# A conditioned transformer block on one core: seven second-level Strassen products in three ff residuals, none in the ssm residuals

## The chip, the core and the metric

The kernel runs on one core of a Trainium2 chip, in fp32. The core has TensorE (PE in the profile), VectorE (DVE), ScalarE (ACT) and GpSimd (POOL), each with a queue of its own, and SyncE (SP), from whose queue most DMAs are issued. An engine takes its instructions strictly in the order in which the program lists them. The metric is the device time of one execution in microseconds (us).

## The reference

Two sequences of 2048 tokens with 512 channels, `x` (2, 2048, 512); each has a row of conditions `t` of 512 numbers, from which six rows of shift, scale and gate are made.

```python
emb = dot(silu(t), ada_w) + ada_b
shift_msa, scale_msa, gate_msa, shift_mlp, scale_mlp, gate_mlp = split(emb, 6)
norm = ln(x) * (1 + scale_msa) + shift_msa
h = gelu(dot(norm, ssm_w1) + ssm_b1)              # 512 x 512, exact gelu
x = x + gate_msa * (dot(h, ssm_w2) + ssm_b2)      # 512 x 512
norm2 = ln(x) * (1 + scale_mlp) + shift_mlp
hf = gelu_tanh(dot(norm2, ff_w1) + ff_b1)         # 512 x 1024
return x + gate_mlp * (dot(hf, ff_w2) + ff_b2)    # 1024 x 512
```

Tokens depend on each other in nothing. The gates differ for the two sequences and are multiplied into the second weights (`w2`, `fw2`), which are therefore loaded and folded twice, once for each sequence.

## The kernel before

**Blocks and stages.** The 4096 tokens are cut into eight blocks of 512 (0 to 3 belong to the first sequence, 4 to 7 to the second). Each block has four matmul stages, and the names of tiles in the profile carry them: *hA* is the ssm hidden product (class `First`), *oA* the ssm residual, *hC* the ff hidden product (class `Second`, `products`), *oC* the ff residual. A loop over i from 1 to 7 puts the stages of neighbouring blocks in turn: hC of block i, oA of block i+1, oC of block i, hA of block i+2. While PE multiplies for one block, the other engines normalize, transpose and form sums for another.

**Strassen-Winograd.** A plain product of two matrices cut into quarters takes eight products of quarters. The Winograd form takes seven, P1 to P7, and pays with sums: four of each operand beforehand (`sums_of_first` for activations, `sums_of_second` for weights, which both give the third and fourth sum as the third and fourth entry of a list), and adds of the results, which DVE makes from PSUM into `x` in place (`residual`, L795). A product of quarters is P1, P2 and so on in the code, and several of them accumulate in one PSUM bank. The banks' tags are y, x, v and t, each with two buffers. At the start of a residual two banks are filled by ACT with the bias row (`seed`), so that the bias comes with the first add. After P1 ACT copies bank y to a new bank x (the order named CARRIED).

**The second level.** In a residual, a product can itself be done by the same form: its quarter matrices are cut into quarters again, and seven *leaves* of 128 columns are multiplied instead of eight. The leaves of the several products that are done so run in rounds: round 0 computes leaf P1 of each of these products, round 1 leaf P2, and so on in the order of `LEAVES`; after a round (but for round 0) DVE adds the results to `x`. Before the change, the ff residuals of blocks 1 to 7 do five of their seven products in leaves (`residual_in_leaves`: P2, P3, P4, P5 and P7; P1 and P6 are plain, L897 the plain matmul, L945 that of a leaf, L959 the adds of leaves). The ssm residuals of blocks 3 to 6 (i from 2 to 5) do P2, P3 and P4 in leaves (`residual_with_leaves`: L832 plain, L847 leaf, L862 adds of leaves), the others none (L495 in `group`, the matmul of `residual` and `First`). The leaf sums of activations are made by POOL on line L349 (a line of `cut_sum`), in the constant tile `forms`, which also holds the registers of the ff hidden product.

**The ff hidden product** has a longer table of sums (`HK_P`, `HK_A`, `HK_B`) and 26 products, which DVE (L1140) and ACT (L1137) collect. Its operands are made by POOL ahead of it from the 'registers' of the normalized block (L1047).

**The order of the work** is written by hand: there is no scheduler. A stage is a list of matmuls, and a dictionary `hooks` says after which product (a number for hC; P1, P2, R0 and so on for the others) the operations of other engines are put into their queues. Whatever the place, each engine takes its own operations in the order of the code, so a hook's place decides what an operation stands behind on its engine. A hook at P5 of a CARRIED stage stands at the place of the fourth product of the usual order.

**The layer norm of a block** goes through these steps: statistics on DVE (L533) or ACT, `root` (a variance on DVE, L603, and a power of -1/2 on POOL, L575), `steps` or `rest` (five small operations on DVE, L607 to L611), `normal` on ACT (L626), `turn` on DVE (L637, a transpose within 32x32 blocks), `move` (16 DMAs, L646), `moved` (ACT's modulate, L669, in place) and at last the sums of the result on POOL.

**Loads.** The tiles of x, h and the normalized blocks come from one pool of seven buffers (`big_tile`); a new tile takes a buffer that became free. `load_x` (L203) brings in a block's x, `load_half` (L221) half of `fw2`, both on SP. Block 4 begins the second sequence. For it `w2` is loaded again and folded with the new gate at i = 2 (`refold2`), and `fw2` at i = 3 (`refold5`; folds on DVE, L397); the bias rows are multiplied by the gates in `gate_bias` (L1023, with L478 for the difference of its halves).

## Time and profile before

| what | value |
|---|---|
| median of three runs | 586.86 us (586.22 to 587.11) |
| profiled execution | 585.99 us |
| its span | 584.2 us |
| PE busy | 576.8 us, 3375 instructions |
| DVE busy | 447.3 us, 891 instructions |
| POOL busy | 422.0 us, 462 instructions |
| ACT busy | 274.1 us, 512 instructions |

The span runs from the first to the last instruction in the trace, the execution's time a little around it. An engine that is busy for nearly all of the span sets the time as long as it isn't kept waiting, so the wait of that engine is what to look for. In a line of the timeline the first number is the start in us from the beginning of the span, the second the length of the group of like instructions in a row, then the engine, the line of the kernel, the operation, the tile written and the tiles read, their shapes, and how many instructions the group has; in square brackets stand idle time just before and what ended it. In a line of groups, the numbers behind the bar are the busy time of all in us and the mean of one in ns. The steady stages of the loop begin, in PE's timeline, at 153.77 (oA of block 2), 165.86 (oC of block 1), 200.78 (hC of block 2), 223.23 (oA of block 3), 234.83 (oC of block 2), 257.37 (hA of block 4), 304.18 (oC of block 3), 326.71 (hA of block 5), 361.31 (oA of block 5) and 454.28 (oC of block 5).

### The profile page before, as it was taken

To read this page: it belongs to the slowest core of one execution; us is meant where nothing else is said; L and a number is where in the kernel's file an instruction comes from. 1 tells how busy PE (TensorE), PEld (TensorE's weight loads), DVE (VectorE), ACT (ScalarE), POOL (GpSimd) and SP (SyncE) were. 2 spreads that over 40 slices of the span, in tenths; PEclk is the share of its full clock that TensorE was granted. 3 is DMA by queue.
4 is the path that set the end of the run, shared out by engine and by line. 5 is a ranking of instruction groups with operands and counts; after the bars stand their busy time and mean duration, and the time that the engine had idled before them with its cause. 6 is when DMAs were issued, how large, how long until landed. Compare 5 with 4: busy or idle time off the path is not lost.

```text
span 584.2 us, 9795 instructions
## 1 busy us (share of the span) xinstructions
PE 576.8 (99%) x3375; PEld 516.4 (88%) x3375; DVE 447.3 (77%) x891; ACT 274.1 (47%) x512; POOL 422.0 (72%) x462
## 2 busy tenths in 40 slices
PE   8999999999999999999999999999999999999996
PEld 5888888888889889998899988998889998899896
DVE  4978898996878576896967678986766487887676
ACT  2234357705642655535733588235665331732520
POOL 1875349999949788599968999997770593369350
PEclk9999999999999999999999999999999999999999
DMA  8990422302205303353032920252130240031002
GB/s 317 395 383 6 109 65 82 108 37 108 56 19 144 145 1 69 116 168 119 1 92 59 312 81 22 51 136 105 49 73 2 96 121 1 0 74 73 0 1 74
DMA packets 25246, 56.52 MB, mean 97 GB/s; under 512 B 4672, under 2 KB 5740, under 8 KB 23532
## 3 DMA queue, kind: packets, MB, share of 16 engines
q1 hardware_dynamic: 21856, 51.67, 27.7%
q10 hardware_dynamic: 3340, 4.22, 2.9%
q8 instruction: 27, 0.44, 0.3%
q14 instruction: 23, 0.19, 0.1%
HBM read 32.80 MB, written 8.40 MB: 71 GB/s over the span
## 4 chain that ended last, share of the span: by engine, by line
PE 92%; DVE 3%; DMA 2%; POOL 1%; issue 1%; SPq 0%; ACT 0%; DVEq 0%; POOLq 0%
PE px_hC L1123 10%; PE py_hA L495 9%; PE py_oC L897 8%; PE pv_hC L1123 8%; PE py_hC L1123 8%; PE pl_oC_P_y L945 8%; PE py_oA L495 5%; PE pl_oC_P_v L945 5%; PE pv_hA L495 4%; PE py_oA L832 3%; PE pl_oC_P_x L945 3%; PE pv_oA L495 2%; PE py_hC L495 2%; PE py_oC L495 2%; PE px_hA L495 2%; PE pv_oC L945 2%
## 5 line engine op out<-in xcount | busy, mean ns | idle before, releaser
L575 POOL TENSOR_TENSOR r<-ve,minus_half 128x4 f32<-128x4 f32 x16 | 16.6, 1036 | 60.5 <-DVE pl_oC_P_v L603 34.0
L669 ACT ACTIVATE nT<-nT,mod,mod 128x512 f32<-128x512 f32 x32 | 23.4, 804 | 57.6 <-DMA nT<-blocks 34.6
L1047 POOL TENSOR_TENSOR forms<-forms 128x256 f32<-128x256 f32 x56 | 42.1, 752 | 4.2 <-DVE forms L1043 0.7
L532 DVE BATCH_NORM_STATS2 st<-x 128x6 f32<-128x512 f32 x56 | 37.9, 677 | 4.9 <-DMA x<-in_x_dram 4.7
L1123 PE MATMUL py_hC<-forms,fw 128*128 128x256 f32 x168 | 41.2, 380 | 0.4 <-DVE hClo L1140 0.4
L349 POOL TENSOR_TENSOR hSC<-hClo,hChi 128x512 f32<-128x512 f32 (+1 forms) x16 | 19.0, 1192 | 26.4 <-ACT hChi L1118 22.9
L1140 DVE TENSOR_TENSOR hClo<-hClo,py_hC 128x512 f32<-128x512 f32 x42 | 28.6, 684 | 11.0 <-ACT hClo L1137 8.5
L1123 PEld LDWEIGHTS py_hC<-forms,fw 128*128 128x128 f32 x168 | 31.6, 190 | 5.4 <-DVE hClo L1140 1.0
L669 ACT ACTIVATE x<-x,mod,mod 128x512 f32<-128x512 f32 x24 | 17.6, 802 | 34.3 <-DMA x<-blocks 34.3
L1140 DVE TENSOR_TENSOR hChi<-hChi,pv_hC 128x512 f32<-128x512 f32 x35 | 23.2, 680 | 8.0 <-PE pv_hC L1123 6.5
L1118 ACT ACTIVATE hClo<-hClo,colsT 128x256 f32<-128x256 f32 x56 | 25.3, 499 | 5.0 <-DVE hClo L1140 4.8
L1123 PE MATMUL px_hC<-forms,fw 128*128 128x256 f32 x112 | 27.6, 379 | 0.0
L626 ACT ACTIVATE nT<-x,nmr,rstd 128x512 f32<-128x512 f32 x32 | 23.7, 804 | 6.2 <-POOL nmr L590 3.7
L959 DVE TENSOR_TENSOR x<-pl_oC_P_y,x 128x256 f32<-128x256 f32 (+1 forms) x66 | 24.7, 374 | 2.2 <-PE pl_oC_P_y L945 0.6
L637 DVE STREAM_TRANSPOSE blocks<-nT 128x512 f32<-128x512 f32 x32 | 22.4, 708 | 5.0 <-ACT nT L626 5.0
L1118 ACT ACTIVATE hChi<-hChi,colsT 128x256 f32<-128x256 f32 x56 | 25.1, 496 | 1.9 <-DVE hChi L1140 1.9
L1137 ACT ACTIVATE hClo<-px_hC 128x512 f32<-128x512 f32 x21 | 12.5, 596 | 28.1 <-PE px_hC L1123 22.7
L897 PE MATMUL py_oC<-fw_s,hSC 128*128 128x256 f32 x112 | 25.3, 379 | 0.0
L897 PE MATMUL py_oC<-fw,hClo 128*128 128x256 f32 x112 | 25.3, 379 | 0.0
L349 POOL TENSOR_TENSOR hClo<-hClo 128x512 f32<-128x512 f32 (+1 forms) x23 | 24.8, 1082 | 0.0
L1123 PEld LDWEIGHTS px_hC<-forms,fw 128*128 128x128 f32 x112 | 21.3, 190 | 2.9
L959 DVE TENSOR_TENSOR x<-pl_oC_P_v,x 128x256 f32<-128x256 f32 (+1 forms) x56 | 20.3, 385 | 4.1 <-PE pl_oC_P_v L945 2.6
(403 smaller groups left out, 1839.2 us busy)
## 6 DMA issues: line engine op xcount, KB each, us to landing
x<-in_x_dram SPq DMA_DIRECT2D x13, 1024.0 KB
out_dram<-x SPq DMA_DIRECT2D x14, 512.0 KB
ada<-in_L_cond_ada_w_dram SPq DMA_DIRECT2D x6, 1024.0 KB
x<-blocks SPq DMA_DIRECT2D x96, 64.0 KB
nT<-blocks SPq DMA_DIRECT2D x80, 64.0 KB
fw<-in_L_cond_ff_w_dram SPq DMA_DIRECT2D x2, 2048.0 KB
w<-in_L_cond_ssm_w_dram SPq DMA_DIRECT2D x3, 1024.0 KB
nT<-blocks ACTq DMA_DIRECT2D x48, 64.0 KB
```

Of the source, the lines that this page charges most:

```text
L349: eng.tensor_tensor(out[:, r], a[:, r], b[:, r], f)
L495: nc.tensor.matmul(ps[b][j * apart][:, j, :], lhs(p, j, k), rhs(p, j, k), start=(fresh and j * (not apart) == 0 and k == 0), stop=(p in (" ...
L532: nc.vector.bn_stats(st, xs[self.i][:, c, :])
L626: nc.scalar.activation(t, x_c, AF.Identity, bias=self.nmr[:, c : c + 1], scale=self.rstd[:, c : c + 1])
L669: nc.scalar.activation(dst, src, AF.Identity, bias=shift, scale=scale)
L897: yield lambda j=j, k=k: nc.tensor.matmul(ps[BANK[p]][:, j, :], hops(p, j, k), wops[p][:, k, :], start=False, stop=(k == kdim - 1), skip_g ...
L945: nc.tensor.matmul(t[:, n, :], hops.leaves[p][f][:, k, :], leaf_wops[p][f][:, k, :], start=room not in started, stop=(f in ("P2", "P3", "P ...
L959: nc.vector.tensor_tensor(d, src, d, ALU.add)
L1047: eng.tensor_tensor(reg[d], reg[a], reg[b], ALU.add if f == "+" else ALU.subtract)
L1118: nc.scalar.activation(h, h, AF.Gelu_apprx_tanh, bias=fb1T[:, m : m + 1])
L1123: nc.tensor.matmul(ps[b][:, j, :], fa[ra][:, j * P : (j + 1) * P], fb[rb].rearrange("p a (c q) -> p c a q", q=Q), start=(fresh and j == 0) ...
L1140: nc.vector.tensor_tensor(dest(d), dest(d), ps[b], op)
```

## The change

Three of the ff residuals, those of blocks 2, 3 and 5 (`SEVEN`), do all seven products in leaves, in a new function; the other ff residuals keep five. All ssm residuals are plain again, so that the leaf sums for `w2` and for the ssm activations go. What the new residual needs is placed anew:

- `residual_in_all_leaves` has two groups of banks, A for P2, P4, P3, P6 and B for P5, P1, P7. In each round the leaves of A are multiplied, then those of B; DVE adds three times for A and five times for B. ACT copies round 0's banks for round 1. Hooks have names such as 0a and 2b, the round and the group.
- Four sums of the weights' quarters P1 and P6 are added. They are made in block 1's arrangement and again after the reload of `fw2`; the fourth ones are kept in room beside the leaf sums of h, which is a big tile (in block 5 the tile of `w1`), and parked in DRAM between blocks 2 and 3. The third sum is made in place in the weight and changes it for the plain use; `plain` takes that back in the blocks that come next with five products.
- Leaf sums of activations: those of P1 and P7 together (`pair_leaf_sums` on half 0), of P2 and P4 (on half 1), and of P5, P6 and P3 (`third_leaf_sums`), all on POOL.
- In these blocks the load of x three blocks on goes to the end of the residual (6b instead of P5), the store of the first half too. In block 2, `w2` is loaded at 0a instead of P1, and its folds and sums move from the residual to the hidden stage that follows and to the next ff hidden stage (`late_w2`), with the gate taken from PSUM.
- `moved` of block i+2 stands at P1 instead of R0 in the one ssm residual (i = 5) that is followed by hA.
- A hook of the folds of `fw2` after the reload goes from places 0 and 8 of the ff hidden stage to 8 alone.

The diff, cut to its core:

```diff
+        fourths, plain = [], []
+        for j, (p, w) in enumerate((("P1", lo[:, :, : D // 2]), ("P6", s[:, 1]))):
+            q, t = {n: v[:, :, 0, :] for n, v in views(w).items()}, [pair_w[:, 0, j], pair_w[:, 1, j], None]
+            ops[p] = second_operands(q, t)
+            sums[p] = sums_of_second(q, t, engs[p])[:3]
+            fourths.append((p, q["21"], t[1]))
+            plain.append(lambda q=q: nc.gpsimd.tensor_tensor(q["12"], q["22"], q["12"], ALU.subtract))
...
+    def seed_leaves(i, row):
+        by_e = row.rearrange("p (q e d) -> p q e d", q=2, e=2)
+        for b, tag, src in (("y", "x", by_e[:, :, 0]), ("v", "v", leaf_row)):
+            t = ps_g.tile([P, 3, P], F32, tag=tag, name=f"pl_oC_{i}_B_{b}")
+            seeds[f"oC_{i}", b] = t
+            nc.scalar.copy(t[:, :2], src)
+            nc.scalar.activation(t[:, 2], row[:, :P], AF.Identity, scale=0.0)
...
+    def residual_in_all_leaves(name, i, hops, leaf_wops, hooks, last):
...
+        groups = {"A": ("P2", "P4", "P3", "P6"), "B": ("P5", "P1", "P7")}
...
+        rooms = {("B", b): seeds[name, b] for b in "yv"}
+        for g, b, tag in (("A", "y", "x"), ("A", "x", "y"), ("B", "x", "y"), ("A", "v", "v")):
+            rooms[g, b] = ps_g.tile([P, len(groups[g]), P], F32, tag=tag, name=f"pl_{name}_{g}_{b}")
...
+        for r, f in enumerate(LEAVES):
...
+            for n, g in enumerate("AB"):
+                room = rooms[g, b]
+                for p in groups[g]:
+                    leaf(g, p, f)
+                if r == 0:
+                    m = len(groups[g])
+                    nc.scalar.copy(rooms[g, "x"][:, :m], room[:, :m])
+                    started.add((g, "x"))
+                elif g == "A":
+                    add(cross, room[:, 3:])
+                    add(like, room[:, 0:4:3])
+                    add(cross, room[:, 1:3])
+                else:
+                    add(like, room[:, :1])
+                    add(cross, room[:, 1:])
+                    add(last_q, room[:, 1:2])
+                    add(cross, room[:, :1])
+                    add(last_q, room[:, 2:])
+                run(hooks.get(f"{r}{'ab'[n]}", ()))
...
+    SEVEN = (2, 3, 5)
...
-            if i == 2:
-                w2_leaf, late_sums = leaves_of_w2(w2_sb, w2_s, (nc.gpsimd, nc.gpsimd))
-            if i > 1:
-                hook(hooks, (10,), hA[i + 1].leaf_sums(nc.gpsimd))
-            hook(hooks, (10,), late_sums)
...
+            if seven:
+                hook(hooks, (14, 15, 16, 17, 18, 19), wsums16)
+                wsums16 = []
+        if i - 1 in SEVEN and not seven and nxt and i != PER_B:
+            hook(hooks, (3, 5), plain_again)
...
-            hook(hooks, (0, 8), fold[:4])
+            hook(hooks, (8,), fold[:4])
...
-            hook(hooks, ("R0",) if ahead else ("P7",), n1[i + 2].moved())
+            hook(hooks, ("P1",) if ahead else ("P7",), n1[i + 2].moved())
...
-            if i == 1:
-                residual(f"oA_{i + 1}", i + 1, hA[i + 1], w2_ops, KD // 2, hooks, order=CARRIED)
-            else:
-                residual_with_leaves(f"oA_{i + 1}", i + 1, hA[i + 1], w2_ops, w2_leaf, hooks)
+            residual(f"oA_{i + 1}", i + 1, hA[i + 1], w2_ops, KD // 2, hooks, order=CARRIED)
...
+        if seven and nx2:
+            n1_sums = hA[i + 2].summed(nc.gpsimd) if ahead else n1[i + 2].summed(nc.gpsimd)
+            hook(hooks, ("0a",), [lambda: n2[i + 1].root()] + (leaf_fold or [])[:-2] + [lambda: n2[i + 1].rest()])
+            hook(hooks, ("2a", "3a"), (leaf_fold or [])[-2:])
+            hook(hooks, ("0a",), sums17[:2] + [s[2] for s in (sums24, sums356, sums17)] + n1_sums[:1])
+            hook(hooks, ("0a",), [s[3] for s in (sums24, sums356, sums17)] + fourth + n1_sums[1:])
+            hook(hooks, ("0b",), [lambda c=c: n2[i + 1].normal(c) for c in range(C)])
+            hook(hooks, ("1a", "1b", "2a", "2b"), [lambda c=c: n2[i + 1].turn(c) for c in range(C)])
+            hook(hooks, ("2b",), [lambda: n2[i + 1].move((nc.sync, nc.scalar))])
+            hook(hooks, ("3b",), n2[i + 1].moved())
...
+        if seven and i + 3 < NBLK:
+            hook(hooks, ("6b",), [lambda: load_x(i + 3)])
...
+            if seven:
+                hook(hooks, ("P6",), [lambda: found.update(gb2=bias_2())])
+                hook(hooks, ("P6", "P6", "P5", "P5", "P7", "P3", "P3", "P4"), w2_fold[:KD])
+                late_w2 = w2_fold[KD:]
```

More of the change, by code (lines that the diff above doesn't have):

```diff
@@ L429, in leaves_of_weight, with fourth @@
             sums[p] = sums_of_second(q, t, engs[p])
+        fourths, plain = [], []
[5 more added lines that the diff above has]
+            plain.append(lambda q=q: nc.gpsimd.tensor_tensor(q["12"], q["22"], q["12"], ALU.subtract))
+        def fourth(room):
+            for j, (p, a, b) in enumerate(fourths):
+                nc.gpsimd.tensor_tensor(room[:, j], a, b, ALU.subtract)
+        sums["fourth"], sums["plain"] = fourth, plain
         return ops, sums
@@ L1493 @@
                 hook(hooks, ("P1", "P2", "P6", "P5"), fold[5:6] + fold[4:5] + later[:2])
-            oC_seeds = [lambda p=p: seed(f"oC_{i}", gb[5], p, five) for p in range(2)]
+            if seven:
+                oC_seeds = [lambda: seed_leaves(i, gb[5])]
+            else:
+                oC_seeds = [lambda p=p: seed(f"oC_{i}", gb[5], p, five) for p in range(2)]
             if not ahead:
```

140 lines of the change are left out of this document (105 added, 35 removed).

## The prediction

> **What bounds the kernel.** I read the page first (busy times, then the chain that ended last), then the timeline of PE, then what PE waited for.
>
> ```profile
> PE 576.8 (99%) x3375; PEld 516.4 (88%) x3375; DVE 447.3 (77%) x891; ACT 274.1 (47%) x512; POOL 422.0 (72%) x462
> PE 92%; DVE 3%; DMA 2%; POOL 1%; issue 1%; SPq 0%; ACT 0%; DVEq 0%; POOLq 0%
> ```
>
> PE is busy for 99% of the span and carries 92% of the chain. So there are only two questions: does the change alter the number or the pace of matmuls, and does it make PE wait. The next lines are from the timeline of PE: start, length, group. Each matmul of the program shows as two instructions.
>
> ```profile
> 153.77 1.89 PE L495 MATMUL py_oA<-w,hA 128*128 128x256 f32 x8
> 155.50 1.89 PE L495 MATMUL pv_oA<-w_s,hSA 128*128 128x256 f32 x8
> 165.86 3.62 PE L897 MATMUL py_oC<-fw,hClo 128*128 128x256 f32 x16
> 169.31 0.61 PE L945 MATMUL pl_oC_P_y<-fw,hChi 128*128 128x128 f32 x4
> 169.75 0.61 PE L945 MATMUL pl_oC_P_y<-fw,hSC 128*128 128x128 f32 x4
> ...
> 223.23 1.89 PE L832 MATMUL py_oA<-w,hA 128*128 128x256 f32 x8
> ...
> 234.83 1.03 PE L897 MATMUL py_oC<-fw,hClo 128*128 128x256 f32 x4
> ...
> 257.37 0.81 PE L495 MATMUL py_hA<-x,w 128*128 128x256 f32 x3
> ...
> 304.18 2.11 PE L897 MATMUL py_oC<-fw,hClo 128*128 128x256 f32 x9
> ```
>
> Starts follow each other without holes: 16 wide instructions take 169.31 - 165.86 = 3.45 us (216 ns each), four narrow ones 0.44 to 0.45 us. What PE waited for between 60 and 574 us is two lines of the view of waits, and their places in its timeline are these:
>
> ```profile
> PE py_hC L1123 <- DVE hClo L1140: 0.4, 1, 0.4
> PE pl_oA_y L847 <- DVE x L862: 0.3, 1, 0.3
> 282.12 1.13 PE L1123 MATMUL py_hC<-forms,fw 128*128 128x256 f32 x4 [0.41 <-DVE hClo L1140]
> 369.62 0.49 PE L847 MATMUL pl_oA_y<-w,hA 128*128 128x128 f32 x2 [0.29 <-DVE x L862]
> ```
>
> With the slack of the matmul before and a slow first one behind (four wide ones take 1.13 here, 1.03 at 234.83), I put the first at about 0.6 to 0.7 us and the second, from its length and the gap, at 0.5 to 0.6. That is all that a change outside the start and the end of the kernel can win back: about 1.2 us.
>
> **The change, part by part.**
>
> *Matmuls.* A product of the ff residual costs 3.45 us plain. As seven leaves it has 28 narrow instructions: 7 x 0.445 = 3.12 us. Two more products in three blocks: 6 x 0.33 = 2.0 us won. The ssm residual takes 234.83 - 223.23 = 11.60 us with leaves and 165.86 - 153.77 = 12.09 us plain; it goes back to plain in four blocks (3 to 6): 4 x 0.49 = 2.0 us lost. Sum: 0.0. Both sides move 168 narrow and 96 wide instructions, so any other price for them gives zero too.
>
> *Vector work in the ff residual (blocks 2, 3, 5).* Before, a block has 27 adds into x; now six rounds of eight: two groups A and B, A with three adds of 256 columns, B with three of 256 and two of 128. A PE round is now 7 x 0.445 = 3.12 us (A 1.78, B 1.34). A bank is written again two rounds later, so the adds of a group in round r must end before that group starts in round r+2. Prices from the DVE timeline of block 2 and the groups by line and shape:
>
> ```profile
> 253.08 0.42 DVE L959 TENSOR_TENSOR x<-pl_oC_P_y,x 128x256 f32<-128x256 f32 x1
> 253.60 0.42 DVE L959 TENSOR_TENSOR x<-pv_oC,x 128x256 f32<-128x256 f32 x1
> 253.94 0.74 DVE L959 TENSOR_TENSOR x<-pl_oC_P_y,x 128x128 f32<-128x128 f32 x2
> 254.59 0.41 DVE L959 TENSOR_TENSOR x<-pl_oC_P_v,x 128x256 f32<-128x256 f32 x1
> L959 DVE TENSOR_TENSOR x<-pl_oC_P_y,x 128x128 f32<-128x128 f32 x22 | 6.2, 282 | 0.6 <-PE pl_oC_P_y L945 0.6
> ```
>
> An add of 256 lasts 0.42, but the next starts 0.34 after it (253.60 to 253.94); with an extra wait the step is 0.52. I take 0.34 each, 0.28 for 128 columns, 0.10 for one wait per group: A 1.12, B 1.68, a round 2.80, under PE's 3.12. Before the first round DVE ends the statistics of the ssm residual and the scales. Block 1, whose ssm residual is plain already, shows it:
>
> ```profile
> 166.06 0.69 DVE L795 TENSOR_TENSOR x<-py_oA,x 128x512 f32<-128x512 f32 x1
> 168.97 0.18 DVE L533 BATCH_NORM_AGGREGATE mv<-st 128x2 f32<-128x6 f32 x1
> 171.58 0.17 DVE L607 TENSOR_TENSOR pl_oC_P_v<-r,pl_oC_P_v 128x4 f32<-128x4 f32 x1 [0.38 <-POOL r L575]
> 172.27 0.15 DVE L611 SCALAR_TENSOR_TENSOR nmr<-mv,pl_oC_P_v 128x4 f32<-128x4 f32 x1
> 173.30 2.83 DVE L637 STREAM_TRANSPOSE blocks<-nT 128x512 f32<-128x512 f32 x4 [0.88 <-ACT nT L626]
> ```
>
> Counted from the stage's first matmul (165.86): statistics end at 3.3, the variance (0.16) and POOL's power (1.02, below) at 4.6, five small steps (0.84) at 5.4. Then, with a turn of 0.71 (2.83 / 4) behind each group of rounds 1 and 2: round 1A ends at 6.5, 1B at 8.9, 2A at 10.7, 2B at 13.1, the last turn at 13.8, 3A at 14.9, 3B at 16.6, 4A at 17.7, 4B at 19.4, 6B at 25.0. PE wants the banks of 3A at 15.6, 3B at 17.4, 4A at 18.7, 4B at 20.5: margins of 0.7, 0.8, 1.0, 1.1. Cost 0. By full lengths (A 1.36, B 1.92, a round 3.28) 3A ends at 16.2 and the waits add to about 0.9 us in blocks 2 and 3; in block 5 a whole hidden stage lies between the statistics and this residual. So bounds 0 and +1.8; I take 0, since the nearest rows are such adds and start early. DVE ends 3.2 us after PE, which the hidden stage behind it (few adds, banks read by round 5 first) takes up.
>
> *POOL.* Leaf sums of h for the ssm residual and for w2 go; sums for P1, P6 and P2, P4 wide and three P's at once come. Block 2 before:
>
> ```profile
> 231.52 1.27 POOL L349 TENSOR_TENSOR forms<-forms,hChi 128x512 f32<-128x512 f32 x1
> 239.91 1.02 POOL L575 TENSOR_TENSOR r<-ve,minus_half 128x4 f32<-128x4 f32 x1 [7.12 <-DVE pl_oC_P_v L603]
> 247.45 0.72 POOL L349 TENSOR_TENSOR hClo<-hClo 128x256 f32<-128x256 f32 x1
> 256.72 1.18 POOL L1047 TENSOR_TENSOR forms<-nT 128x256 f32<-128x256 f32 x1
> ```
>
> The idle 7.1 us before the power takes the first two sums of 768 columns (estimate 1.8 each, from 0.72 and 1.27). From the power's end at 4.6: two sums of P1/P7 to 7.1; thirds (1.27, 1.8, 1.27) to 11.5; one sum for the next hidden stage to 12.8; fourths to 14.1, 15.9, 17.2; two weight sums to 18.6; three more sums to 22.4. Round 5 reads the 768-wide fourth in its third product, at 15.6 + 0.9 = 16.5: margin 0.6, the smallest. Cost 0; if the power comes at 5.1 as in block 2 before (239.91 - 234.83, behind adds that are gone), 1.0 per block. Register sums start some 2 us later than 21.9 (256.72), since turns now sit between adds; the 12 us of a hidden stage and the first products of the next one cover them.
>
> *ACT at the stage's start.* The first leaf round comes at once instead of behind 3.45 us of a plain product, and round 1 needs ACT's copy of round 0's bank. ACT may still be at the modulates of the block after, which wait for SP's transpose DMAs:
>
> ```profile
> 292.02 11.25 SPq L646 DMA_DIRECT2D x<-blocks  x16
> 305.07 2.93 ACT L669 ACTIVATE x<-x,mod,mod 128x512 f32<-128x512 f32 x4 [8.67 <-DMA x<-blocks]
> 307.91 0.36 ACT L927 COPY pl_oC_P_v<-leaf_row 128x256 f32<-128x256 f32 x1
> 234.63 2.93 ACT L669 ACTIVATE x<-x,mod,mod 128x512 f32<-128x512 f32 x4 [7.59 <-DMA x<-blocks]
> ```
>
> In block 3 the stage will start 0.49 us later, at 304.67; ACT is free at 307.91 = 3.2, a copy of 512 columns ends at about 3.8 (estimate 0.6: 0.36 at 256, and more), round 1 wants it at 3.1: **+0.7 us**. In block 2 ACT is free 2.1 us into the stage (237.5 against 235.3): the copy ends at 2.8, 0. If the issue of its 16 DMAs takes the 11.25 us of block 3 there as well, up to 0.7; bounds 0 and +1.4, taken 0.7.
>
> *Queues.* The load of the x three blocks on moves to the end of the residual, into a buffer that only the last leaf round frees, and on SP everything behind it waits. In block 3 that is both halves of fw2:
>
> ```profile
> 321.51 0.54 SPq L203 DMA_DIRECT2D x<-in_x_dram  x1
> 323.34 1.72 SPq L221 DMA_DIRECT2D fw<-in_L_cond_ff_w_dram  x2
> 330.09 2.48 DVE L397 TENSOR_TENSOR fw<-fw,pgate 128x512 f32<-128x512 f32 x4 [2.43 <-DMA fw<-in_L_cond_ff_w_dram]
> 339.96 0.42 DVE L478 TENSOR_TENSOR gb<-gb 128x256 f32<-128x256 f32 x1
> ```
>
> x goes out 2.2 us before the stage's end instead of 5.2 (326.7 - 321.5), so the folds start some 3 us later; the slack of the lines behind them leaves about 2 us at 339.96. The next stage's first bank that waits for a DVE add is taken 6.05 us (28 x 0.216) after that stage starts, and I find 0.7 us left. Bounds 0 and +1.3; taken 0, by the idle 2.43 and what follows it. The w2 reload, its folds and the park DMA lie in stages where DVE and SP have room: 0. The late x of block 2 is read 6.9 us after it is issued at the earliest: 0.
>
> *Waits that go.* The wait at 369.62 is in the leaf form of the ssm residual, where DVE was late; plain, a bank has a product of 1.73 us between its uses: -0.56, bounds -0.56 and 0. The one at 282.12 follows the gate bias of ssm, one line of which takes 1.17 at that place and 0.42 at 339.96; it stays where it was: 0, bounds -0.65 and 0.
>
> ```profile
> 278.75 1.17 DVE L478 TENSOR_TENSOR gb<-gb 128x256 f32<-128x256 f32 x1
> ```
>
> *Sum.* 0.0 + 0.7 - 0.56 = +0.14 us. The profiled execution took 585.99 (span 584.2 and 1.8 around it), so 586.1; the median of the three runs is 0.87 above that execution: **587.0**.
>
> **Rivals.**
>
> 1. *DVE becomes the bound of the new residual* (slower, the other side). It decides as soon as a round of eight adds takes more than about 2.9 us; at full lengths it takes 3.28. For it: 27 adds become 48, and 253.08 to 253.60 is a step of 0.52. Against it: the steps of 0.34. Time: 587.0 + 1.8 = 588.8. The Trainium skill, "VectorE: DVE Perf Modes", section "The DRAIN you can't avoid", says that the next operation does not start until the pipe is empty; by that rule each add costs its full length and this rival holds. This trace does not agree for adds without a wait: 253.94 starts 0.08 us before the add at 253.60 ends.
>
> 2. *POOL and the late loads* (slower): the power at 5.1 gives 1.0 in blocks 2 and 3, the late fw2 up to 1.3, some of both waits shared: +2.5, 589.5. For it: margins of 0.6 and 0.7 in a chain of fifteen operations. Against: POOL had 7.1 us idle before the power.
>
> 3. *Both old waits go and no new one comes* (faster): -0.56 - 0.65, 585.6. For it: POOL loses the w2 leaf sums in that very stage. Against: the 2.93 us of ACT above, and the bias line stays.
>
> **How the numbers follow.** Forecast 0.50, rival 1 0.22, rival 2 0.20, rival 3 0.08. About what a measurement of this kernel can tell from no change is 0.2%, 1.2 us: the forecast and its own range (586.2 to 588.0) lie inside, rivals 1 and 2 above, rival 3 just below. So faster 0.08, same 0.50, slower 0.42. The range leaves out rival 3 and the worst of rival 2: 585.8 to 590.0.
>
> **What would show it.** In the profile after: PE with the same 3375 instructions; ff residuals of blocks 2, 3, 5 at 21.9 us plus their waits; the ssm residuals at 12.1; no wait of PE for DVE x at the sixth block; a wait of some 0.7 us for ACT's copy after the first round in block 3. Waits of PE for DVE x in rounds 5 and 6 would prove rival 1, for POOL's forms or leaves rival 2. I am wrong if one of these stages is more than 1 us longer than its matmuls, or if a hidden stage behind one shows waits.

## The result, and the profile after

The changed kernel takes 589.27 us (median of 6 runs, 587.82 to 590.34), the kernel before 586.27 on the same chip: a ratio of 1.0049, 95% interval 1.0038 to 1.0060. It is slower by 3.0 us, and its runs lie 2.5 us apart where those of before lie 0.9 apart. The profiled execution took 588.81 us with a span of 586.8, 2.6 more than before.

The busy times and the chain that ended last, of the changed kernel:

```profile
PE 577.3 (98%) x3375; PEld 515.8 (88%) x3375; DVE 443.0 (75%) x912; ACT 273.6 (47%) x509; POOL 420.3 (72%) x431
PE 84%; DVE 4%; DMA 4%; ACT 3%; SPq 2%; issue 2%; POOL 1%; DVEq 0%; POOLq 0%; ACTq 0%
```

PE has the same 3375 instructions and the same busy time within 0.5 us. Its share of the chain fell from 92% to 84%: the time came from waiting, not from multiplying. The view of PE's waits between 60 and 574 us (in all, times, longest):

```profile
PE pl_oC_A_x L1060 <- ACT pl_oC_A_x L1086: 1.0, 1, 1.0
PE py_hA L520 <- DVE hA L782: 0.7, 1, 0.7
PE pv_oA L520 <- ACT pv_oA L484: 0.4, 1, 0.4
PE py_hA L520 <- POOL forms L1128: 0.3, 1, 0.3
```

Their places in PE's timeline, with a fifth at 238.70 that shows as a slow first matmul only:

```profile
238.70 0.71 PE L1060 MATMUL pl_oC_A_x<-fw,hChi 128*128 128x128 f32 x4
268.34 1.53 PE L520 MATMUL py_hA<-nS,w 128*128 128x256 f32 x6 [0.25 <-POOL forms L1128]
309.02 0.71 PE L1060 MATMUL pl_oC_A_x<-fw,hChi 128*128 128x128 f32 x4 [1.04 <-ACT pl_oC_A_x L1086]
339.11 1.75 PE L520 MATMUL py_hA<-nS,w 128*128 128x256 f32 x7 [0.70 <-DVE hA L782]
481.27 1.56 PE L520 MATMUL pv_oA<-w_s,hSA 128*128 128x256 f32 x6 [0.42 <-ACT pv_oA L484]
```

None of the five is in a place where the kernel before had one; the two old ones are gone. What each costs is best read as the length of its stage, from the stage's first matmul in PE's timeline to that of the next one. In us:

```
stage                     before  changed  difference
oA 3, 4, 6 (each)          11.59    12.09    +0.50
oA 5                       12.15    12.09    -0.06
oC 2 (seven products)      22.54    22.25    -0.29
hA 4                       12.09    12.58    +0.49
hC 3                       23.13    22.47    -0.66
oC 3 (seven products)      22.54    23.19    +0.65
hA 5                       12.09    13.03    +0.94
hC 4                       22.50    22.75    +0.25
oC 5 (seven products)      22.54    21.88    -0.66
oA 7                       12.09    12.78    +0.69
```

They add to +2.8, and PE's last matmul ends 2.8 later (582.65 against 579.84); the other stages agree within 0.04. The ff residual of block 5 is 21.88 long, which is its matmuls and no wait. So the residuals of blocks 2 and 3 hold waits of 0.37 and 1.31.

What stands behind them, in the timelines of the other engines, ACT first:

```profile
305.56 2.93 ACT L694 ACTIVATE x<-x,mod,mod 128x512 f32<-128x512 f32 x4 [8.66 <-DMA gsb<-gates]
308.40 0.57 ACT L1086 COPY pl_oC_A_x<-pl_oC_A_y 128x512 f32<-128x512 f32 x1
477.81 2.93 ACT L694 ACTIVATE nT<-nT,mod,mod 128x512 f32<-128x512 f32 x4 [13.57 <-DMA nT<-blocks]
480.64 0.58 ACT L484 COPY pv_oA<-gb 128x512 f32<-128x512 f32 x1
```

At 309.02, ACT's copy of round 0 stands behind four modulates and ends at 308.97, 0.05 us before PE goes on at 309.02. The modulates wait for DMAs: the view names the load of the gates, which SP issues right behind the 16 transposing DMAs, and in e2 the transposing DMAs themselves. In block 5 the bias row for the next ssm residual (L484) stands behind four other modulates. DVE and, in the last two lines, SP:

```profile
264.30 2.48 DVE L397 TENSOR_TENSOR w<-w,pgate 128x512 f32<-128x512 f32 x4 [0.73 <-ACT pgate L337]
266.70 0.69 DVE L557 BATCH_NORM_STATS2 st<-x 128x6 f32<-128x512 f32 x1
267.52 0.67 DVE L782 TENSOR_TENSOR hA<-py_hA,hA 128x512 f32<-128x512 f32 x1
333.97 2.48 DVE L397 TENSOR_TENSOR fw<-fw,pgate 128x512 f32<-128x512 f32 x4 [4.40 <-DMA fw<-in_L_cond_ff_w_dram]
338.29 0.68 DVE L782 TENSOR_TENSOR hA<-py_hA,hA 128x512 f32<-128x512 f32 x1
292.26 10.30 SPq L671 DMA_DIRECT2D x<-blocks  x16
326.27 0.98 SPq L221 DMA_DIRECT2D fw<-in_L_cond_ff_w_dram  x2
```

In both hidden ssm stages the bank that P4 wants is read by L782, and L782 stands behind folds of weights: those of w2, which the change moved here, and those of fw2, whose load goes out at 326.27 (323.34 before) and whose first fold starts at 333.97 (330.09 before; the stage itself starts only 1.2 us later). The view names POOL and not DVE at 268.34, as one of POOL's sums ends near there too. It isn't POOL that PE waits for: in e2, below, the same sums of POOL come 0.5 us later (267.99 in place of 267.51), L782 0.9 us earlier, and PE doesn't wait.

### The profile page after: what moved, and what is told of

Same layout as the page of the kernel before. It is cut to its first block, busy times and chain, and to the rows that moved or that the text cites. A ratio compares the mean times of both kernels' runs of the same rounds, so it can differ in the third digit from the quotient of the medians.

```text
span 586.8 us, 9773 instructions
## 1 busy us (share of the span) xinstructions
PE 577.3 (98%) x3375; PEld 515.8 (88%) x3375; DVE 443.0 (75%) x912; ACT 273.6 (47%) x509; POOL 420.3 (72%) x431
## 4 chain that ended last, share of the span: by engine, by line
PE 84%; DVE 4%; DMA 4%; ACT 3%; SPq 2%; issue 2%; POOL 1%; DVEq 0%; POOLq 0%; ACTq 0%
PE px_hC L1204 10%; PE py_oA L520 8%; PE py_hC L1204 8%; PE py_hA L520 8%; PE pv_hC L1204 7%; PE py_oC L922 5%; PE pv_oA L520 4%; PE pl_oC_P_y L970 4%; PE pv_hA L520 3%; PE py_hC L520 2%; PE py_oC L520 2%; PE pl_oC_P_v L970 2%; PE pl_oC_A_y L1060 2%; PE px_oA L520 2%; SPq L671 2%; PE px_hA L520 2%
## 5 line engine op out<-in xcount | busy, mean ns | idle before, releaser
L520 PE MATMUL py_oA<-w,hA 128*128 128x256 f32 x112 | 26.5, 379 | 0.0
L349 POOL TENSOR_TENSOR hClo<-hClo 128x512 f32<-128x512 f32 (+1 forms) x23 | 26.2, 1141 | 0.0
L820 DVE TENSOR_TENSOR x<-py_oA,x 128x512 f32<-128x512 f32 x26 | 17.8, 686 | 10.6 <-PE py_oA L520 9.4
L820 DVE TENSOR_TENSOR x<-pv_oA,x 128x512 f32<-128x512 f32 x16 | 11.0, 686 | 17.7 <-PE pv_oA L520 9.0
L520 PEld LDWEIGHTS py_oA<-w,hA 128*128 128x128 f32 x112 | 21.1, 190 | 2.9
```

The costliest lines, as they stand in the source:

```text
L349: eng.tensor_tensor(out[:, r], a[:, r], b[:, r], f)
L520: nc.tensor.matmul(ps[b][j * apart][:, j, :], lhs(p, j, k), rhs(p, j, k), start=(fresh and j * (not apart) == 0 and k == 0), stop=(p in (" ...
L820: nc.vector.tensor_tensor(d, ps[BANK[p]][:, js], d, ALU.add)
```

## The experiments

Behind each run stand the difference of its median to that of the kernel before on the same chip ("+2.0 us") and the ratio with its interval. Single mends of less than 1 us are within the spread of the changed kernel's own runs, so that what follows from them is read from the stages' lengths and not from the medians. The lengths, in us:

```
stage   before changed  e2     e3     e4     e5     e6     e7     e8     e9     e10    e12
oC 2    22.54  22.25   22.32  22.29  22.31  21.88  22.24  22.45  22.54  22.28  21.88  21.88
hA 4    12.09  12.58   12.09  12.58  12.66  13.38  12.09  12.58  12.09  12.09  12.19  12.35
hC 3    23.13  22.47   23.26  22.47  22.47  22.46  23.45  22.47  22.93  22.97  23.29  22.68
oC 3    22.54  23.19   21.88  23.84  23.23  21.88  23.74  23.39  22.54  23.25  21.88  21.88
hA 5    12.09  13.03   13.16  12.09  13.34  13.35  12.86  13.49  12.09  12.97  12.09  12.09
oA 7    12.09  12.78   12.65  12.54  12.92  13.08  13.00  12.09  12.09  13.23  12.09  12.09
oC 4    22.54  22.54   22.98  22.97  22.98  22.54  22.54  22.54  22.98  22.54  22.53  22.54
```

### ACT's order at the start of the new residual (e1, e5)

In blocks 2 and 3 the modulates of the block after move from the ssm residual to the new ff residual:

```diff
-            hook(hooks, ("P1",) if ahead else ("P7",), n1[i + 2].moved())
+            if ahead or not seven:
+                hook(hooks, ("P1",) if ahead else ("P7",), n1[i + 2].moved())
...
+            if not ahead:
+                hook(hooks, ("0b",), n1[i + 2].moved())
             hook(hooks, ("0b",), [lambda c=c: n2[i + 1].normal(c) for c in range(C)])
```

> The changed kernel, with ACT's four modulates of the block after (blocks 2 and 3) put behind the copies of round 0, where they stood ahead of them. Theory (ACT's order makes round 1 wait): the waits of PE at 238.70 (0.36 us) and 309.02 (1.30 us) go, nothing takes their place, the kernel is 1.6 us faster than the changed one: about +1.3 us against the kernel before. Rival (the normalization behind the modulates comes about 1 us later, DVE's turns with it, and DVE's adds then hold up rounds 3 to 5): a wait for DVE x of about 1 us in each of the two blocks, and no gain: +3 us.

Measured: 621.79 us, 1.0603 (1.0588 to 1.0617). In this form POOL's sums of the same block (hook 0a) stand ahead of the modulates in the program, so the sums are of the block before modulation, and the modulates wait for POOL to have read it. Neither theory said that. ACT waits 16.87 us for POOL, the normalization behind it too, DVE stands in front of a turn for 17.85 us, and the adds behind the turn hold two banks. From the timelines of ACT and DVE:

```profile
255.98 2.93 ACT L694 ACTIVATE x<-x,mod,mod 128x512 f32<-128x512 f32 x4 [16.87 <-POOL x L349]
259.65 0.71 DVE L662 STREAM_TRANSPOSE blocks<-nT 128x512 f32<-128x512 f32 x1 [17.85 <-ACT nT L651]
```

And from the view of PE's waits:

```profile
PE pl_oC_A_y L1060 <- DVE x L1078: 29.6, 2, 15.5
```

One hook in the wrong order went through ACT and DVE to PE. The edit was made again with the sums behind the modulates:

```diff
-            hook(hooks, ("0a",), sums17[:2] + [s[2] for s in (sums24, sums356, sums17)] + n1_sums[:1])
-            hook(hooks, ("0a",), [s[3] for s in (sums24, sums356, sums17)] + fourth + n1_sums[1:])
+            after_copy = "0a" if ahead else "0b"
+            if not ahead:
+                hook(hooks, ("0b",), n1[i + 2].moved())
+            hook(hooks, (after_copy,), sums17[:2] + [s[2] for s in (sums24, sums356, sums17)] + n1_sums[:1])
+            hook(hooks, (after_copy,), [s[3] for s in (sums24, sums356, sums17)] + fourth + n1_sums[1:])
```

> As the run with the modulates behind round 0's copies, but POOL's leaf sums and the sums of the modulated block stand behind the modulates in the program (hook 0b in place of 0a, POOL's own order unchanged), so that POOL sums the modulated block. Theory (ACT's order makes round 1 wait): the waits of PE at the first matmul of round 1 in blocks 2 and 3 (0.36 and 1.30 us in the changed kernel) go: about +1.4 us against the kernel before. Rival (the normalization of the next block, then at 6.5 in place of 5.5 us into the stage, makes DVE late for rounds 4 and 5): PE waits for DVE x in blocks 2 and 3, about 1 us in each, +2.5 to +3 us.

Measured: 588.44 us, +2.1 (1.0033; 1.0021 to 1.0046). Both residuals take 21.88: ACT's order was the cause of both waits, and no wait of PE for DVE x appears. But the hidden stage behind block 2 grows from 12.58 to 13.38. The timeline of DVE shows how:

```profile
262.36 1.42 DVE L1124 TENSOR_TENSOR forms<-copy,forms 128x256 f32<-128x256 f32 x4 [3.41 <-POOL forms L1128]
264.82 2.48 DVE L397 TENSOR_TENSOR w<-w,pgate 128x512 f32<-128x512 f32 x4 [0.38 <-ACT pgate L337]
268.04 0.66 DVE L782 TENSOR_TENSOR hA<-py_hA,hA 128x512 f32<-128x512 f32 x1
```

The folds start 0.5 us later in the trace than in the changed kernel although PE is 0.3 us ahead. They stand behind register sums (L1124) that wait for work of ACT and POOL on the block normalized one stage earlier, and DVE is idle for 3.41 us in front of those. Of the 1.68 won, 0.80 is lost again.

### The folds of w2 and the old wait at 282 (e2, e6, e9)

```diff
-                hook(hooks, ("P6", "P6", "P5", "P5", "P7", "P3", "P3", "P4"), w2_fold[:KD])
+                hook(hooks, ("P7", "P3", "P3", "P4"), w2_fold[:KD])
```

> The changed kernel, with the four folds of w2 in the hidden ssm stage of block 4 put behind the add of P7. Theory (the folds delay DVE's add L782, which P4's bank waits for): the wait at 268.34 (0.49 us) goes and stays gone: about +2.5 us against the kernel before. Rival (the 0.49 us is only the old wait of the ff hidden stage behind, at 282.12 in the kernel before, taken earlier): PE then waits about 0.5 us near 282 again, and the time stays at +3.0 us.

Measured: 588.28 us, +1.85 (1.0033; 1.0022 to 1.0045). The hidden stage of block 4 is back at 12.09, and the ff hidden stage behind it at 23.26, from PE's timeline:

```profile
282.59 0.70 PE L1204 MATMUL py_hC<-forms,fw 128*128 128x256 f32 x2 [0.48 <-DVE hClo L1221]
```

By the stages the rival holds: the wait of the hidden stage goes, and one near 282 is there again. The two stages together make 35.22 before, 35.05 in the changed kernel and 35.35 here. But it is not one wait that is taken at one place or the other (in e5 the two stages make 35.84). The one near 282 goes with the length of one operation of DVE among its reads, the difference of the halves of the gate bias (L503, L478 before). From DVE's and POOL's timelines, the changed kernel and then e2:

```profile
278.38 1.28 POOL L349 TENSOR_TENSOR w_s<-w,w_s 128x512 f32<-128x512 f32 x1
279.43 0.51 DVE L503 TENSOR_TENSOR gb<-gb 128x256 f32<-128x256 f32 x1
```

```profile
278.82 1.27 POOL L349 TENSOR_TENSOR w_s<-w,w_s 128x512 f32<-128x512 f32 x1
279.15 1.23 DVE L503 TENSOR_TENSOR gb<-gb 128x256 f32<-128x256 f32 x1
```

Each time DVE's operation ends 0.28 or 0.29 us after POOL's (the last section shows more of this), so its length depends on where it meets POOL's. With the bias in this place it takes 1.17 before, 0.51 in the changed kernel (0.50 or 0.51 in e3, e4, e5 and e7), 1.23 here and 0.97 in e8; hC 3 is 0.68, 0.02, 0.81 and 0.48 above the 22.45 of its matmuls. So the old wait went because this operation came at a better moment, and here it is back. (In this profile ACT's modulates of block 3 started at 304.59, and that residual has no wait; the edit doesn't touch them. How long that wait is differs from run to run, 0 to 1.96 us in the columns where ACT's order is that of the changed kernel, with the landing of the DMAs in front of the modulates. No other wait varies as much in the table.)

Then the multiply of the gate bias was put earlier, with the folds as in e2:

```diff
-            hook(hooks, (8,), late_bias)
+            hook(hooks, (1,), late_bias)
```

> The w2 folds put behind the add of P7 as before, and the multiply of the ssm gate bias moved in the ff hidden stage of block 3 from the place behind its 9th product to that behind its 2nd. Theory (PE waits near 282 because DVE makes the gate bias, 0.68 us and up to 1.17 us, among its reads of the products): both the wait at 268 and that at 282 go, about +1.8 to +2.0 us against the kernel before, 0.6 below the run with the folds alone. Rival (DVE has no room in the first half of that stage): the wait returns at an earlier product, and the time stays at +1.8 to +2.5 us with a wait of 0.5 us or more between 270 and 285.

Measured: 589.85 us, +3.5 (1.0055; 1.0041 to 1.0069). The rival again: 23.45, with waits at 276.45 and 277.77 in place of 282, although the bias's difference takes only 0.42 there. At last the folds were put where DVE stands idle:

```diff
-            hook(hooks, (8,), late_bias)
+            hook(hooks, (1,), late_bias)
...
-            gate_2 = (lambda: gate[2, b]) if seven else gate_rows[2, b]
+            gate_2 = gate_rows[2, b]
...
+        if refold2 and seven:
+            hook(hooks, ("P1",), w2_fold[:KD])
         hook(hooks, ("P1",), [begin])
...
-                hook(hooks, ("P6", "P6", "P5", "P5", "P7", "P3", "P3", "P4"), w2_fold[:KD])
```

> The changed kernel, with the four folds of w2 at the head of DVE's queue in the hidden ssm stage of block 4 (hook P1, ahead of the register sums that wait for ACT's copies, with the gate from SBUF), and the multiply of the gate bias behind the 2nd product of the ff hidden stage that follows. Theory (DVE has 2 to 3 us idle at that stage's start, which the 2.4 us of folds fill): the stage takes 12.09 in place of 12.58, the ff hidden stage of block 3 stays at 22.47: about +2.4 us against the kernel before. Rival (POOL's register sums and DVE's folds of two SBUF inputs hold each other up, and the work only passes on): 12.09 but 22.9 or more in the ff hidden stage, +3 us.

Measured: 589.69 us, +3.1 (1.0054; 1.0040 to 1.0068). The hidden ssm stage takes 12.09; the ff hidden stage 22.97, so the rival's number. What the rival said of the folds shows as well: with the gate from SBUF they take 4.08 in place of 2.48 us, and POOL's register sums beside them 0.96 to 1.18 in place of 0.73:

```profile
259.75 4.08 DVE L397 TENSOR_TENSOR w<-w,gsb 128x512 f32<-128x512 f32 x4
262.11 1.18 POOL L1128 TENSOR_TENSOR forms<-nT 128x256 f32<-128x256 f32 x1
```

Whether the rest of the wait in hC 3 comes from that or from the early bias is not settled: the last run, with the bias elsewhere, has 22.68, and the folds first with the bias in its old place were not run. This profile also has the longest wait for the late bias row in block 7's ssm residual (13.23) and began the first ff hidden stage 0.5 us later than the changed kernel's (71.36 against 70.84), which the edit doesn't touch.

### The load of fw2 (e3)

```diff
-        if seven and i + 3 < NBLK:
+        if seven and i + 3 < NBLK and not refold5:
             hook(hooks, ("6b",), [lambda: load_x(i + 3)])
...
             load_half("fw2", fw2, fw2_sb, 0)
+            if seven:
+                load_x(i + 3)
```

> The changed kernel, with the load of x of block 6 put behind both halves of fw2 on SP, where it stood ahead of them. Theory (the folds come late because fw2 does): the first fold starts about 1.5 to 2.5 us earlier than 333.97 and the wait of PE at 339.11 (0.94 us) goes: about +2.1 us against the kernel before. Rival (the folds are late by the order of DVE's own work, and the load has time): the wait keeps more than half of its length, +2.6 to +3.0 us.

Measured: 588.71 us, +2.3 (1.0043; 1.0029 to 1.0056). SP's and DVE's timelines of this run:

```profile
324.81 1.17 SPq L221 DMA_DIRECT2D fw<-in_L_cond_ff_w_dram  x2
326.52 0.34 SPq L203 DMA_DIRECT2D x<-in_x_dram  x1
330.41 2.48 DVE L397 TENSOR_TENSOR fw<-fw,pgate 128x512 f32<-128x512 f32 x4 [0.20 <-DMA fw<-in_L_cond_ff_w_dram]
337.53 0.69 DVE L782 TENSOR_TENSOR hA<-py_hA,hA 128x512 f32<-128x512 f32 x1 [2.81 <-PE py_hA L520]
```

fw2 goes out 1.5 us earlier and its folds start 3.6 us earlier, L782 waits for PE and not PE for it, and the stage is at 12.09. The theory holds, with a larger shift of the folds than the 1.5 to 2.5 us expected. Against the kernel before the time falls by 0.7 only, from +3.0 to +2.3; in this profile the residual of block 3 is 0.65 longer than in the changed kernel's and oC 4 is 0.43 longer, neither of which the edit touches.

### The bias row behind the modulates (e4, e7)

```diff
-            hook(hooks, ("3b",), n2[i + 1].moved())
+            if not ahead:
+                hook(hooks, ("3b",), n2[i + 1].moved())
...
             hook(hooks, ("2a", "6a") if seven else ("R4", "P4"), [lambda p=p: seed(f"oA_{i + 2}", gb[2], p) for p in range(2)])
+            if seven:
+                hook(hooks, ("6a",), n2[i + 1].moved())
```

> The changed kernel, with ACT's modulates in the ff residual of block 5 put behind the seed of the next ssm residual, where they stood ahead of it. Theory (the seed stands behind modulates that wait for their DMAs): the wait at 481.27 (0.69 us) goes, about +2.3 us against the kernel before. Rival (the modulates, now later, hold up POOL's register sums and with them the ff hidden stage of block 6): a new wait of PE at 491 to 514 of 0.5 us or more, +2.8 to +3.2 us.

Measured: 588.92 us, +2.5 (1.0046; 1.0033 to 1.0058). The wait at 481 is gone, and 6 us later there is one as long:

```profile
484.13 1.42 DVE L1124 TENSOR_TENSOR forms<-copy,forms 128x256 f32<-128x256 f32 x4 [2.56 <-POOL forms L1128]
486.13 0.68 DVE L820 TENSOR_TENSOR x<-pv_oA,x 128x512 f32<-128x512 f32 x1
487.56 0.67 PE L520 MATMUL py_oA<-w,hA 128*128 128x256 f32 x2 [0.59 <-DVE x L820]
```

The rival is right that the delay passes on, though it comes in the ssm residual and not in the ff hidden stage: the register sums wait for the late modulates, and the residual's adds stand behind them on DVE. So it is not the order on ACT but the late modulates, and they are late because the transposing DMAs start only when the fourth turn is done:

```diff
-            hook(hooks, ("1a", "1b", "2a", "2b"), [lambda c=c: n2[i + 1].turn(c) for c in range(C)])
-            hook(hooks, ("2b",), [lambda: n2[i + 1].move((nc.sync, nc.scalar))])
+            hook(hooks, ("1a",) if ahead else ("1a", "1b", "2a", "2b"), [lambda c=c: n2[i + 1].turn(c) for c in range(C)])
+            hook(hooks, ("1a",) if ahead else ("2b",), [lambda: n2[i + 1].move((nc.sync, nc.scalar))])
```

> The changed kernel, with the four turns of the next block in the ff residual of block 5 all behind round 1's first group (hook 1a), where they stood one behind each group of rounds 1 and 2; the DMAs of the move follow them. Theory (the modulates are late because the turns are spread out): the 16 DMAs begin near 466.5 in place of 469.5, the modulates near 475 in place of 477.8, and the wait of PE for the seed at 481.27 (0.69 us) goes without one in the ssm residual behind it: about +2.3 us against the kernel before. Rival (2.1 us of turns put into round 1 make DVE late): PE waits for DVE x in round 4 of block 5, 0.5 us or more, and nothing is won, +3 us.

Measured: 589.09 us, +2.7 (1.0044; 1.0032 to 1.0057). The modulates start at 475.85 in place of 477.81, the ssm residual is at 12.09 and the ff residual still at 21.88, with no wait for DVE x: the theory holds for this wait. The time is above the +2.3 expected; in this profile oC 3 (23.39) and hA 5 (13.49) are longer than in the changed kernel's.

### The two halves of the change (e8)

```diff
-    SEVEN = (2, 3, 5)
+    SEVEN = ()
```

> The set of blocks with seven products in leaves is empty: only the ssm residuals are changed, from three products in leaves to plain in blocks 3 to 6, with the ff residuals at five in all blocks. By the prediction: four stages of ssm residual at 12.09 in place of 11.60 us, +1.96; the wait at 369.62 goes, -0.56; the one at 282.12 stays: +1.4 us against the kernel before. Rival (the leaf sums that POOL no longer makes also free DVE's gate bias): the wait at 282.12 goes too, +0.8 us. The rest up to the changed kernel's +3.0 is then what the ff residual with seven products costs with its waits, although its matmuls are 1.96 us shorter.

Measured: 588.37 us, +2.0 (1.0031; 1.0020 to 1.0043). The four ssm residuals are at 12.09 (+1.44 with the wait of oA 5 gone), as the prediction had it. hC 3 is at 22.93, so 0.48 of the 0.68 of that wait is still there: neither theory, nearer to the first (the bias's difference takes 0.97, see e2). The rest is not from the ssm residuals: 0.44 in oC 4 (hardware, below), and this run's first ff hidden stage began 0.83 later (71.66 against 70.83). By the medians, then, the ff half of the change, which saves 1.98 of matmuls, costs about 1 us. By the stages' lengths, without the two that are not from the ssm residuals, it costs 1.6 (2.8 less 1.44, and 0.20 for hC 3).

### All mends, and the margin of DVE (e10, e11, e12)

The edits of e5, e9, e3 and e7 together:

> Four mends in one: modulates behind round 0's copies with the sums behind them, folds of w2 first and the bias early, fw2 before x, and the turns of block 5 at once. Theory (each wait has its own cause and each is taken away): ff residuals of blocks 2, 3 and 5 at 21.88, all ssm stages at 12.09, the ff hidden stage of block 3 at 22.47: against the kernel before +1.44 for the ssm residuals, -1.98 for the ff residuals, -0.66 for that hidden stage, together -1.2 us (0.998). Rival (the waits come from DVE and ACT chains that the change made longer, and return in the next stage): one or more hidden stages 0.5 us or more above those numbers, 0 to +1.5 us.

Measured: 585.67 us, -0.9 (0.9986; 0.9978 to 0.9995), and 11 runs within 0.9 us. All three ff residuals are at 21.88 and the ssm stages at 12.09 to 12.19. One thing went as the rival said: hC 3 is at 23.29. The bias stands between the first reads:

```profile
271.33 1.28 DVE L1221 TENSOR_TENSOR hChi<-hChi,pv_hC 128x512 f32<-128x512 f32 x2 [1.14 <-PE pv_hC L1204]
272.54 0.68 DVE L1104 TENSOR_TENSOR gb<-pgate,gb 128x512 f32<-128x512 f32 x1
273.25 1.07 DVE L503 TENSOR_TENSOR gb<-gb 128x256 f32<-128x256 f32 x1
```

On top of this kernel the rounds were made longer on DVE:

```diff
                     add(last_q, room[:, 2:])
+                    for _ in range(2):
+                        add(cross, room[:, 1:])
```

> The four mends, and in each of rounds 1 to 6 of the three ff residuals with seven products two further adds of 256 columns on DVE (one of group B's adds made three times, so that what is added to x is not the residual). By the adds' measured step of 0.33 us a round goes from 2.55 to 3.2 us on DVE, above PE's 3.12. Theory (DVE had room, and rival 1 of the prediction decides only above about 2.9 us a round): now the turns' 2.8 us are not caught up, PE waits for DVE x in rounds 4 to 6, 0.5 to 2.5 us a block, +2 to +6 us over the run of the mends. Rival (an add takes its full length of 0.41, so the room was nil before): PE waits for DVE x in the run of the mends already, and here 3 us or more a block.

Measured: 592.64 us, +7.0 over e10 (1.0103 to the kernel before; 1.0087 to 1.0120). A round as it is, in the changed kernel, is the first fence; with two more adds, the second:

```profile
318.36 1.05 DVE L1078 TENSOR_TENSOR x<-pl_oC_A_v,x 128x256 f32<-128x256 f32 x3
319.33 1.47 DVE L1078 TENSOR_TENSOR x<-pl_oC_B_v,x 128x256 f32<-128x256 f32 x5
320.72 1.07 DVE L1078 TENSOR_TENSOR x<-pl_oC_A_y,x 128x256 f32<-128x256 f32 x3
```

```profile
253.90 1.09 DVE L1078 TENSOR_TENSOR x<-pl_oC_A_y,x 128x256 f32<-128x256 f32 x3
254.90 2.26 DVE L1078 TENSOR_TENSOR x<-pl_oC_B_y,x 128x256 f32<-128x256 f32 x7
257.07 1.08 DVE L1078 TENSOR_TENSOR x<-pl_oC_A_v,x 128x256 f32<-128x256 f32 x3
```

A round lasts 2.36 us on DVE (318.36 to 320.72) where PE takes 3.12, and 3.17 with ten adds. Then PE waits: the residuals of blocks 2 and 3 take 23.23 (+1.35). More is lost behind them: DVE ends its adds late, and hA 4 takes 14.41 (+2.2), oA 7 13.42 (+1.3). The theory holds in kind and for blocks 2 and 3; block 5 loses only 0.14, and the total is above its range, as it left out what comes behind.

Last, the bias at the end of the hidden ssm stage, in DVE's 1.14 us of idle time:

```diff
+        if refold2 and seven:
+            hook(hooks, ("P4",), [lambda: found["gb2"]()])
+            late_bias = []
```

> The four mends, with the multiply of the ssm gate bias at the end of the hidden ssm stage of block 4, ahead of the first reads of the ff hidden stage, where the run of the mends has it behind the first two reads. Theory (the bias, 1.8 us there, delays the reads behind it; DVE has 1.1 us idle ahead of the first read): the ff hidden stage of block 3 takes 22.45 to 22.6 in place of 23.29, and the kernel is 0.7 to 0.8 us faster than the run of the mends: -1.6 us against the kernel before (0.997). Rival (the reads come late wherever the bias stands in the first half of that stage): the stage stays at 23 us or more, -0.9 us.

Measured: 585.40 us, -1.1 (0.9979; 0.9970 to 0.9988), 11 runs from 584.91 to 585.74. The two hidden stages together go from 35.48 to 35.03 (12.35 and 22.68), so 0.45 of the 0.7 to 0.8 expected. The page's chain of this kernel:

```profile
PE 95%; DVE 2%; DMA 2%; issue 0%; SPq 0%; DVEq 0%
```

The view of waits lists nothing for PE between 60 and 574 us. This kernel is faster than both: 0.2% below the kernel before, and 4.1 us below the change as it was made, each taken against the kernel before on its own chip (-1.1 and +3.0).

## Why the prediction was right or wrong

The range (585.8 to 590.0) holds 589.27. The likeliest case, no measurable change at 587.0, was wrong: the kernel is slower by 0.49%, to which side 0.42 had been given. The sum forecast +0.14 us where +3.0 was measured. Two signs that the prediction named for its being wrong came: the residual of block 3 is 1.31 longer than its matmuls, and the hidden stages behind blocks 2 and 3 show waits. That the range holds the time is in part luck, since its upper part was there for rivals 1 and 2, and most of what they put there didn't happen. By its steps:

- *Matmuls, 0.0*: right. 2.00 lost in four ssm residuals, 1.98 won in three ff residuals (22.54 to 21.88).
- *Vector work, 0*: right, and with more room than stated: a round takes 2.36 on DVE, where 2.80 was reckoned, since an add of 128 columns steps by 0.20 and not 0.28 and no wait was left between the groups. Rival 1 (588.8) is near to the measured time and nevertheless false: no PE wait for DVE x stands in any of the three residuals. Its bound of about 2.9 us a round fits the runs, 2.36 without a wait and 3.17 with ten adds and waits (e11), but no run lies near it; its price for an add, the full length, was not what the adds cost.
- *POOL, 0*: right. No wait for forms or leaves in the new residuals.
- *ACT at the stage's start, +0.7*: the right mechanism, the wrong size. It is 0.37 in block 2, taken as 0, and 1.31 in block 3, together 1.68 and above the upper end of 1.4. The step took ACT's time of before (free at 307.91) for the time after. SP issues the 16 transposing DMAs no later than before, the last by 302.56 (303.27 before), but the modulates start 3.0 us after that in place of 1.8, and ACT is free at 308.49; in block 2 they start 2.3 us after it in place of 1.7. In the runs that leave this place as it is, it is 1.7 us (e2) to 3.65 us (e3). Why the last DMAs land so late stays open. New in block 3 is the load of the parked sums, which SP issues behind the gates; e2 has it too, and no run takes it out and leaves the rest.
- *Queues, 0*: this is the step that failed most. The late fw2 was priced in hC 4 with 0.7 us of margin. It cost 0.94 in hA 5, one stage earlier, where the add L782 stands behind the folds, and 0.25 in hC 4. The bound of +1.3 held it; the value taken didn't. And the 0 for the reload of w2, its folds and the park DMA, "in stages where DVE and SP have room", was a sum of busy time, not a look at the order: DVE had room at the start of hA 4, in front of the register sums, and none where the folds were put (+0.49).
- *Waits that go*: the one at 369.62 went with -0.56, as said. The one at 282.12 was said to stay and is not to be found: the line of the gate bias that takes 1.17 before takes 0.51 in the changed kernel. The prediction saw that this line takes 1.17 at one place and 0.42 at another, but didn't ask why; e2 shows that it depends on where the line meets an operation of POOL. With the new wait in hA 4, the two stages together changed by -0.17 only.
- *Not in the prediction*: the bias row of oA 7, +0.69. The ordering of ACT was looked at where the residual starts and not where it ends.

Rival 2 (589.5) had the time nearly right and one of its two causes, the late fw2. The others, the modulates and the folds of w2, it did not have.

## What to carry to other kernels

When PE is busy for 99% and a change keeps its matmuls equal, the change is priced by where each moved operation now stands in its engine's queue. For each one, ask which instruction behind it hands a bank to PE, and how late that one is; the sum of busy time says nothing about it. And a wait that disappears from a trace is not yet won: here it hung on where two engines' operations met, and came back when another wait was mended. Add up the stages on both sides of it, and look at what it hung on, before counting it.

## What the runs showed of the hardware

The length of a DVE operation with both inputs in SBUF follows POOL. The same line, `fw<-fw` with 256 columns, takes 0.41 in one execution and 1.58 in another. Changed kernel, DVE and POOL, and then e2:

```profile
391.89 0.41 DVE L349 TENSOR_TENSOR fw<-fw 128x256 f32<-128x256 f32 x1
391.94 1.50 POOL L349 TENSOR_TENSOR nS<-x 128x512 f32<-128x512 f32 x1
```

```profile
391.18 1.58 DVE L349 TENSOR_TENSOR fw<-fw 128x256 f32<-128x256 f32 x1
391.21 1.26 POOL L349 TENSOR_TENSOR nS<-x 128x512 f32<-128x512 f32 x1
```

In e2 DVE's operation ends at 392.76, 0.29 us after POOL's at 392.47. The gate bias of the kernel before (278.75 to 279.92) ends 0.29 after a POOL operation that runs from 278.35 to 279.63. In the changed kernel DVE was first, and POOL's operation took 1.50 in place of 1.26. So either engine waits for the other's instruction to end. The Trainium skill, "SBUF — State Buffer", section "Who interferes with whom", says the same: a DVE instruction with two SBUF inputs contends with a GpSimd instruction that reads SBUF, and the ports that they share are an exclusive lock. In e1 to e4, e8 and e11 this came out to DVE's loss (1.58 or 1.59), and oC 4 took 22.97 or 22.98; where the line takes 0.41 or 0.42, as in the changed kernel, and 0.83 before, it took 22.53 or 22.54. Which engine gets in when both come within 0.05 us of each other, the traces don't tell.

Adds with one input in PSUM follow each other in less than their length, 0.33 us apart at 0.41 long. Adds of 128 columns are 0.20 apart at 0.28 long. The prediction weighed a section of the Trainium skill by which they would not; that section points to another of the same page, "VectorE: DVE Perf Modes", "Two Vector instructions with no wait between them", by which only certain instructions, which it calls held, wait until all earlier ones have finished, and the trace agrees.
